# Two value tiles ahead of the branch, and another order of requests at the start of a decoder's last layer

## The chip, the cores and the metric

The kernel runs on one core of a Trainium2 chip. A core has a matrix engine (TensorE, PE in the profile), a vector engine (VectorE, DVE), a scalar engine (ScalarE, ACT), a programmable engine (GpSimd, POOL) and a sync engine (SyncE, SP). Each runs its own list of instructions in order and waits on semaphores for the others. SP, ACT and POOL also request transfers (DMA) between memory and the on-chip buffers. TensorE writes its results into eight banks of PSUM, from which ScalarE or VectorE must read them before a bank can be used again.

The metric is the device time of one launch in microseconds (us), lower is better. One of the launches was recorded by the hardware profiler; its times are what the profile shows.

## The reference

A decoder of two layers on a batch of 4 sequences with 512 positions and 256 features, everything in 32-bit floats. After each step the input is added and a layer normalisation follows.

```python
x = _layernorm(x + _L0_attn_ref(...))    # layer 0: a recurrence that learns on the fly
x = _layernorm(x + _L0_xattn_ref(...))   # attention over a context of 1601 positions
x = _layernorm(x + _L0_ffn_ref(...))     # 8 experts, the best two for each position
x = _layernorm(x + _L1_attn_ref(...))    # layer 1: causal self attention, 16 heads of 16
x = _layernorm(x + _L1_xattn_ref(...))   # attention over the context, 16 heads, rotary
x = _layernorm(x + _L1_ffn_ref(...))     # a feed-forward block with quantised weights
```

Of these the change touches the start of layer 1. There the self attention of a batch entry needs its keys, queries and values from x, and the cross attention needs, from the context, values and keys; the keys are rotated with two tables, a cosine and a sine:

```python
K = (key @ Wk.T + bk).reshape(b, sk, H, D).transpose(0, 2, 1, 3)
V = (value @ Wv.T + bv).reshape(b, sk, H, D).transpose(0, 2, 1, 3)
...
K = apply_rope(K, cos_k, sin_k)      # x * cos + x2 * sin, x2: neighbours swapped
...
scores = jnp.einsum('bqhd,bkhd->bhqk', Q, K) * SCALE
...
out = jnp.einsum('bhqk,bkhd->bqhd', attn, V)
```

The context does not depend on x, so its values and keys can be made at any time before the cross attention.

## The kernel before, in words

**The experts and the branch.** The experts of layer 0 run block by block in `run` (L1248), with side work (`attention_first`, L1158) that loads the weights of layer 1, the context of batch entry 0 (transposed, into the tiles `qt` and `ks`, which serve as store for it until they are needed), and two tiles `vself` for self-attention values, with columns of ones and zeros already set. A last function, `rest` (L1297), holds further blocks behind a condition on the number of expert rows (L1299); in this input the condition is false. Behind it comes a second condition with two versions of `last_layer` (L1311). So each engine passes two branches between the last expert block and layer 1.

**The start of the last layer** (L1952 to L1977) is written out by hand; within an engine the instructions keep the order of the program. In this order:

- the rows of the experts' results for batch entries 0 and 1 are gathered by POOL (L1371, 16 gathers);
- the 13 value tiles of batch entry 0 are made from the context (`context(0, (), range(4), ...)`): two products of 128 x 256 on TensorE into a PSUM bank, and a copy by ScalarE (L1506) into `vals[0]`. They are read when the cross attention begins;
- ScalarE loads its table for exponentials (L1963);
- the list `order` (L1973): the first two key products of entry 0 (`keys0[0:2]`, ScalarE adds a bias, L1492), the sum and the normalisation of x (`add`: VectorE's L1385, L165, L170, then ScalarE's L134, L136, L180), the key product `keys0[4]`, the transposes of x (`turn`: L1406, copied by ScalarE, L1409), the keys and queries of the first heads (`k0_`, `q0_`, L1431; they go to memory, through SP and ACT, L1340), the key product `keys0[5]`, and the rows of these keys and queries, fetched from memory in the layout of the scores (`rows0`, SP, L1343);
- the rotation of these four key tiles by VectorE (`turns0`), each with its store (L1340, `kcd<-raw`); the self-attention values of entry 0 (L1450); eight value tiles of entry 1.

**The units.** Then 32 units follow, one for each group of four heads of a batch entry, first the self attention of all entries, then the cross attention. A unit has a pass for the maxima of the scores (`slot1`, matmuls into tiles `most`, reduced by VectorE, L1588), which runs ahead of its main pass (scores L1627, exponentials on ScalarE L1637, weighted sums L1662). The maxima of a unit go through four small transfers (L1616, `qt<-nrows`) into the queries' rows. Other work is cut into pieces and slipped in between (`extras`). The first list (L1980) holds the second half of entry 0's keys and queries (`k1_`, `q1_`), the key products `keys0[2:4]`, `keys0[6]` and `keys0[7]` (rotated by POOL, L1459 to L1461), the stores still owed (`flush(0)`) and behind them the four rows of `rows1` (L1343), and value tiles of entry 1, whose context comes in chunks that ScalarE requests two ahead (`chunk`, L1471, L1476). Before unit 0's main pass SP requests the rotation tables (L2025 to L2027, `c_cos`, `c_sin`, 800.5 KB each).

**What orders the requests.** SP's list is strictly in order: a request that must wait holds up those behind it. In the compiled program the transfers of SP and ACT take turns on eight landing counters, in the order in which they stand in the program, both engines together. A request waits until the transfer that last used its counter, eight requests earlier, has landed.

```python
extras[0] = [
    k1_, q1_, *keys0[2:4], lambda: (keys0[6](), keys0[7]()), lambda: (flush(0), rows1()),
    *values1[8:11],
] + extras[0]
```

Of the kernel before, what the change touches and what calls it, by code (L numbers as in the profile page):

```python
# [9 lines left out]
F32 = mybir.dt.float32  # L10
# [7 lines left out]
P = 128  # L18
B, S, D = 4, 512, 256
S2 = 1601  # L20
NT = S // P
NKT = (S2 + P - 1) // P
# [3 lines left out]
NH, HD = 16, 16  # L26
# [4 lines left out]
MASKED = -float(2.0**100)  # L31
NLEV = 7
LEADX = 6
AHEAD = 20
PACE = 1.2
BOUNDED = 5000.0
# [7 lines left out]
def decoder(ctx: ExitStack, tc: tile.TileContext, a: dict, out: bass.AP):  # L44
    nc = tc.nc
# [16 lines left out]
    def bank():  # L62
        return psum["B"].tile([P, 512], F32, tag="bank", name="bank")
# [150 lines left out]
    def mm(ps, terms):  # L214

        n = len(terms)
        for i, (l, r) in enumerate(terms):
            nc.tensor.matmul(ps, l, r, start=(i == 0), stop=(i == n - 1))  # L218
# [52 lines left out]
    with (  # L271
# [248 lines left out]
        going, waiting, turn = [ttt(0)], [1, 2, 3], 0  # L520
# [283 lines left out]
    VW = HD + 1  # L804
# [4 lines left out]
    with tc.tile_pool(name="p2", bufs=2) as p2, ExitStack() as ordered:  # L809
# [102 lines left out]
        xaV = weight(p2, "xaV")  # L912
# [33 lines left out]
        for i in range(len(steps) + 1):  # L946
            if i + 1 < len(steps):
                b, t = steps[i + 1]
# [11 lines left out]
            if i > 0:  # L960
                b, t = steps[i - 1]
# [53 lines left out]
            pool.tile([P, n + 1], F32, tag=f"{name}{g}", name=f"{name}{g}")[:, :n] for g in range(NG)  # L1015
        ]

    def values_tile(pool, name, n, eng=nc.gpsimd):
        t = pool.tile([P, n, NH * VW + HD - 1], F32, tag=name, name=name)
        eng.memset(t[:, :, NH * VW :], 0.0)  # L1020
        heads = t[:, :, : NH * VW].rearrange("p k (h r) -> p k h r", r=VW)
        eng.memset(heads[:, :, :, HD : HD + 1], 1.0)
        return t


    with tc.tile_pool(name="p3", bufs=2) as p3, ExitStack() as ordered:
        W = {}
# [263 lines left out]
        run(blocks, more)  # L1291
        for _ in more:
            pass
        ordered.close()


# [14 lines left out]
    def last_layer(causal):  # L1311

        with ExitStack() as s4:
# [16 lines left out]
                ready[k] for k in ("diagq", "later", "qt", "ks", "nms", "vself")  # L1330
            )
            pv0 = s4.enter_context(tc.tile_pool(name="pv0", bufs=1, side="right"))
            vals = [values_tile(pv0, "v0", NKT, nc.vector)]
            kcross = [
                p4c.tile([P, S2 + 1], F32, tag=f"kc{i}", name=f"kc{i}")[:, :S2] for i in range(3)
            ]
# [128 lines left out]
            def flush(n):  # L1465
                while len(going) > n:
                    going.pop(0)()
# [14 lines left out]
            def context(b, keys, values, here=None):  # L1482


                def key(src, i, c, eng, apart=None):
                    if apart is None:
                        flush(1)
                    k0, kw = chunks[i]
                    ps = one()
                    mm(ps[:, :kw], [(W["xaK"][:, h, c * P : (c + 1) * P], src()[h][:, :kw]) for h in range(2)])  # L1490
                    raw = raw_tile()
                    nc.scalar.activation(raw[:, :kw], ps[:, :kw], AF.Identity, bias=ready["bk"][:, c : c + 1])  # L1492
                    turn = lambda: rotated(raw, kw, slice(k0, k0 + kw), eng, ready["turn", i] if here else None)
                    write = lambda: to_rows(kcd[b], c, k0, kw, raw[:, :kw])
                    if apart is None:
                        turn()
                        going.append(write)
                    else:
                        apart.append(lambda: (turn(), write()))

                def value(src, k):
                    kn, c0 = kn_of(k), (k % 4) * P
                    ps = one()[:, :D]
                    mm(ps[:kn], [(src()[c][:, c0 : c0 + kn], W["xaV"][:, c, :]) for c in range(2)])
                    dst = vals[b % 2][:kn, k, : NH * VW].rearrange("p (h r) -> p h r", r=VW)
                    nc.scalar.copy(dst[:, :, :HD], ps[:kn].rearrange("p (h r) -> p h r", r=HD))  # L1506

                items = []
                for i in sorted({*keys, *values}):
                    if here is None:  # L1510
                        src = lambda n=len(stream): chunk(n)
                        stream.append((b, i))
                    else:
                        src = lambda i=i: here[2 * i : 2 * i + 2]
                    eng = nc.gpsimd if here is None or i % 2 else nc.vector
                    if i in keys:
                        items += [
                            lambda *apart, s=src, i=i, c=c, e=eng: key(s, i, c, e, *apart) for c in range(2)
                        ]
                    if i in values:  # L1520
                        items += [lambda s=src, k=k: value(s, k) for k in range(4 * i, min(4 * i + 4, NKT))]
                return items
# [435 lines left out]
                f()  # L1958
            for f in fetch1:
                f()  # L1960
            for f in context(0, (), range(4), here=qt + kself):
                f()
            nc.scalar.preload_act_table_set(EXP_AND_LN)  # L1963


            keys0 = context(0, range(4), (), here=qt + kself)
            (k0_, q0_), rows0 = self_rows(
# [2 lines left out]
            (k1_, q1_), rows1 = self_rows(0, 1)  # L1970
            turns0 = []
            apart = lambda f: lambda: f(turns0)
            order = [apart(f) for f in keys0[0:2]] + add + [apart(keys0[4])] + turn + [k0_, q0_, apart(keys0[5]), rows0]  # L1973
            for f in order:
                f()
            for f in turns0 + self_values(0) + add1 + values1[:8]:
                f()  # L1977
            cosT, sinT = (p4c.tile([P, S2], F32, tag=n, name=n) for n in ("c_cos", "c_sin"))

            extras[0] = [  # L1980
                k1_, q1_, *keys0[2:4], lambda: (keys0[6](), keys0[7]()), lambda: (flush(0), rows1()),
                *values1[8:11],
            ] + extras[0]
            extras[1] = values1[11:] + keys1[:2] + extras[1]
# [27 lines left out]
            for i, u in enumerate(units):  # L2012
                for f in starts[i]:
                    f()
                nk = NKT if u[2] else NT
                work = extras[i]
                ran = 0
                while done["n"] < ends1[u] + lead(u):
                    reduces = [next1() for _ in range(min(2, ends1[u] + lead(u) - done["n"]))]
                    for f in reduces:  # L2020
                        f()
                    prepared()
                    if len(work) > nk // 2:
                        work.pop(0)()
                if i == 0:  # L2025
                    for t, name in ((cosT, "c_cos"), (sinT, "c_sin")):
                        nc.sync.dma_start(t, a[name])  # L2027
                ran = 0
                for k in range(nk):
                    due = (u, k - 1)  # L2030
                    if k == 0:
                        due = (units[i - 1], (NKT if units[i - 1][2] else NT) - 1) if i else None
                    pairs, reduces = [], []
                    for half in range(2):
                        shorter = causal and not u[2] and (k > 1) == (half == 1)
                        if shorter:
                            reduces.append([next1()] if i != 15 or done["n"] < ends1[units[16]] + LEADX else [])
                        pairs.append([scores(u, k, half, h) for h in range(2)])
                        if not shorter:
                            reduces.append([next1()] if i != 15 or done["n"] < ends1[units[16]] + LEADX else [])  # L2040
                        if 9 <= i < 16 and ahead and (i - 9) * NT + k >= PACE * (AHEAD - len(ahead)):
                            reduces[half].append(slot1(*ahead.pop(0)))
                        elif i == 15 and done["n"] < ends1[units[16]] + LEADX:
                            reduces[half].append(next1())
                        if u[2]:
                            exponents(u, k, half, pairs[half])
                            for f in reduces[half]:
                                f()
                            if quiet[i]:
                                quiet[i].pop(0)()  # L2050
                    if not u[2]:
                        for half in range(2):
                            if not causal:
                                diagonal(k, pairs[half])
                            exponents(u, k, half, pairs[half])
                            for f in reduces[half]:
                                f()
                            if quiet[i]:
                                quiet[i].pop(0)()
                    prepared()  # L2060
                    if k and u[2]:
                        weighted(*due)
                    while work and ran * nk < (k + 1) * (ran + len(work)):
                        f = work.pop(0)
                        f()
                        ran += 1
                        if f is pause:
                            break
                    if due and not (k and u[2]):
                        weighted(*due)  # L2070
                while work:
                    work.pop(0)()
                while quiet[i]:
                    quiet[i].pop(0)()
# [172 lines left out]
```

## Time and profile before

| | us |
|---|---|
| device time, three launches | 2027.69, 2021.38, 2018.23 |
| median | 2021.38 |
| profiled execution | 2012.39 |
| its span, first to last instruction | 2010.7 |
| mean granted TensorE clock | 0.99 |
| TensorE busy | 1967.9 (98%) |
| VectorE, ScalarE, POOL busy | 1139.6, 1065.1, 647.4 |
| last expert matmul to first matmul of the last layer | 860.90 to 865.21 |
| first score matmul of unit 0 (`most`) | 903.74 |

The times in the profile are counted from the start of the span. A row of a timeline has start, duration, engine, line, operation, what is written and read, the shapes, how many instructions are merged into the row, and in brackets how long the engine sat idle before it and what ended that. A row of the chain of waits has start, duration and what ran or was waited for. A busy TensorE is not a TensorE at its best: the granted clock (PEclk, 1.00 is full) tells how fast its matmuls run.

### The profile page before, as it was taken

How to read it: one execution, taken by the hardware profiler on the slowest of the kernel's cores; microseconds unless marked ns; L12 is line 12 of the kernel's file. 1: busy time of each engine (PE TensorE's matmuls, PEld its weight loads, DVE VectorE, ACT ScalarE, POOL GpSimd, SP SyncE). 2: the span in 40 equal slices, each digit the busy share in tenths (PEclk: the TensorE clock that was granted, in tenths of full speed). 3: DMA queues.
4: the chain of work that ended last, by engine and by line, in shares of the span. 5: the costliest groups of instructions: out<-in, count | busy, mean ns of one | idle time of the engine just before them, and what ended most of it. 6: DMA issues, size and time to landing. Idle time of an engine off the chain costs nothing.

```text
span 2010.7 us, 33740 instructions
## 1 busy us (share of the span) xinstructions
PE 1967.9 (98%) x12736; PEld 1221.4 (61%) x12736; DVE 1139.6 (57%) x2834; ACT 1065.1 (53%) x2241; POOL 647.4 (32%) x678
## 2 busy tenths in 40 slices
PE   9999999999999999988999999999999999999998
PEld 6768677788899999964455553333433333333366
DVE  3455334452243233356667887777777788887323
ACT  1111222224655555534555567788778788878721
POOL 3010001122222222233733344655655355353110
PEclk9999999999999999999999999999999999999999
DMA  9930411117887786743422110111210120102001
GB/s 366 358 106 1 166 66 54 51 64 278 331 309 278 260 324 261 291 118 117 129 74 66 54 61 28 56 38 48 77 45 29 35 87 18 33 18 85 1 11 34
DMA packets 80110, 242.61 MB, mean 121 GB/s; under 512 B 14135, under 2 KB 37085, under 8 KB 68029
## 3 DMA queue, kind: packets, MB, share of 16 engines
q1 hardware_dynamic: 59148, 141.86, 20.4%
q0 software_dynamic: 13152, 85.64, 11.2%
q10 hardware_dynamic: 7632, 12.80, 2.1%
q8 instruction: 105, 1.72, 0.3%
q14 instruction: 73, 0.59, 0.1%
HBM read 194.47 MB, written 56.69 MB: 125 GB/s over the span
## 4 chain that ended last, share of the span: by engine, by line
PE 50%; DVE 2%; POOL 1%; ACT 1%; DMA 1%; issue 1%; SPq 0%; ACTq 0%; POOLq 0%; DVEq 0%
PE s L1627 13%; PE one L218 12%; PE po L1662 12%; PE most L218 11%; PE one L1693 1%; DVE most L1588 1%; DVE pm L1586 1%; ACT x L180 0%; PE one L1718 0%; ACT ex L1637 0%; DMA kcd<-raw 0%; DVE st L165 0%; POOL raw L1459 0%; POOL swp L1460 0%; POOL raw L1461 0%
## 5 line engine op out<-in xcount | busy, mean ns | idle before, releaser
L1637 ACT ACTIVATE ex<-s 128x512 f32<-128x512 f32 (+4 forms) x1088 | 526.3, 565 | 159.3 <-PE most L218 101.0
L1586 DVE TENSOR_REDUCE pm<-most 128x1 f32<-128x512 f32 x768 | 478.7, 682 | 99.1 <-PE most L218 96.1
L218 PE MATMUL most<-kc,qt 32*128 32x512 f32 (+1 forms) x1920 | 399.4, 533 | 0.8 <-ACT ex L1637 0.2
L1627 PE MATMUL s<-qt,kc 32*128 32x512 f32 (+1 forms) x1560 | 382.0, 617 | 0.0
L1679 POOL TENSOR_TENSOR ot<-ot,part 128x512 f32<-128x512 f32 (+3 forms) x201 | 243.3, 1211 | 290.4 <-ACT part L1678 282.2
L1627 PEld LDWEIGHTS s<-qt,kc 32*128 32x128 f32 (+1 forms) x1560 | 125.0, 181 | 165.8 <-ACT ex L1637 125.5
L1662 PE MATMUL po<-ex,v 128*32 128x512 f32 (+1 forms) x1664 | 225.5, 606 | 0.2
L218 PEld LDWEIGHTS most<-kc,qt 32*128 32x128 f32 x1920 | 157.6, 184 | 45.5 <-issue 16.4
L1109 DVE TENSOR_TENSOR g<-g,sg 128x1024 f32<-128x1024 f32 (+1 forms) x38 | 45.5, 1197 | 214.0 <-ACT sg L1107 214.0
L1588 DVE CUSTOM_DVE_ANT_0 most<-most,c_diagq 128x384 f32<-128x384 f32 (+3 forms) x256 | 119.2, 516 | 45.9 <-PE most L218 44.8
L218 PE MATMUL wide<-xbT,eWg 128*128 128x128 f32 (+1 forms) x928 | 133.7, 304 | 1.5 <-ACT g L1107 1.5
L218 PE MATMUL wide<-xbT,eWi 128*128 128x128 f32 (+1 forms) x928 | 133.9, 304 | 0.0
L218 PE MATMUL bank<-eWo,g 128*128 128x256 f32 x592 | 130.8, 379 | 0.0
L218 PEld LDWEIGHTS wide<-xbT,eWi 128*128 128x128 f32 x928 | 124.9, 191 | 8.0 <-issue 1.1
L218 PEld LDWEIGHTS wide<-xbT,eWg 128*128 128x128 f32 x928 | 124.7, 192 | 8.3 <-ACT g L1107 1.7
L1662 PEld LDWEIGHTS po<-ex,v 128*32 128x32 f32 (+1 forms) x1664 | 34.5, 108 | 149.9 <-ACT ex L1637 145.9
L1678 ACT COPY part<-po 128x512 f32<-128x512 f32 (+3 forms) x201 | 114.4, 569 | 16.9 <-PE po L1662 15.0
L218 PEld LDWEIGHTS bank<-eWo,g 128*128 128x128 f32 x592 | 111.1, 190 | 14.3
L218 PE MATMUL most<-ks,qt 32*128 32x256 f32 (+3 forms) x512 | 95.0, 483 | 6.1 <-ACT v L1506 3.5
L711 POOL DMA_INDIRECT xs<-x,rows x32 | 31.3, 978 | 214.5 <-DVE ltot L697 173.9
L1627 PE MATMUL s<-qt,ks 32*128 32x128 f32 (+3 forms) x512 | 98.1, 482 | 0.9 <-DMA qt<-nrows 0.7
L1640 POOL TENSOR_SCALAR_AFFINE_SELECT ex<-ex 128x256 f32<-128x256 f32 x128 | 51.7, 408 | 128.2 <-ACT ex L1637 127.8
(339 smaller groups left out, 2974.9 us busy)
## 6 DMA issues: line engine op xcount, KB each, us to landing
xs<-zero SPq DMA_DIRECT2D x32, 512.0 KB
kc<-kcd SPq DMA_DIRECT2D x16, 800.5 KB
eWo<-in_eWo SPq DMA_DIRECT2D x8, 1408.0 KB
eWi<-in_eWi SPq DMA_DIRECT2D x8, 1028.0 KB
eWg<-in_eWg SPq DMA_DIRECT2D x8, 1028.0 KB
qt<-qd SPq DMA_DIRECT2D x31, 256.0 KB
ctxT<-in_ctxT SPq DMA_DIRECT2D x4, 1601.0 KB
kcd<-in_c_rowkc SPq DMA_DIRECT2D x4, 1601.0 KB
```

What stands on the lines that cost most here:

```text
L218: nc.tensor.matmul(ps, l, r, start=(i == 0), stop=(i == n - 1))
L711: nc.gpsimd.indirect_dma_start(xs, bass.IndirectOffsetOnAxis(ap=rows[:, k * NT + t : k * NT + t + 1], axis=0), x[b][:, t, :], None)
L1109: nc.vector.tensor_tensor(part, part, dst, ALU.mult)
L1586: nc.vector.tensor_reduce(pm[:, t, j, c : c + 1], ps, AX.X, ALU.max)
L1588: nc.vector.tensor_tensor_reduce(out=ps[:, :n], in0=ps[:, :n], in1=diagq[:, 384 - t * P : 384 - t * P + n], scale=1.0, scalar=LOWEST, op0= ...
L1627: nc.tensor.matmul(ps[:kn, q0:], kt[rows, k * P : k * P + kn], q2[rows, q0:], start=True, stop=cross or causal)
L1637: nc.scalar.activation(ex[:kn, h, q0:], ps[:kn, q0:], AF.Exp)
L1640: nc.gpsimd.affine_select(out=block, in_=block, pattern=[[0, 2], [1, P]], compare_op=ALU.is_ge, fill=0.0, base=0, channel_multiplier=-1,)
L1662: nc.tensor.matmul(po[j * 32 : j * 32 + 32, q0:], (vals if cross else vself)[b % 2][:kn, k, c0 : c0 + 32], ex[:kn, j % 2, q0:], start=True ...
L1678: nc.scalar.copy(part[:, q0:], po[:, q0:])
L1679: nc.gpsimd.tensor_tensor(state["ot"][:, q0:], state["ot"][:, q0:], part[:, q0:], ALU.add)
L1693: nc.tensor.transpose(pt[:, t * P : (t + 1) * P], ot[:, t * P : (t + 1) * P], ident)
```

## The change

There are four edits.

1. The first two value tiles of batch entry 0 (`SOON = 2`) are made at the end of the experts' stage, ahead of both branches, into the second `vself` tile. In the last layer SP copies them from there into `vals[0]`; the loop over value tiles and the memsets of `vals[0]` leave them out.
2. The key product `keys0[5]` moves ahead of the transposes of x, from behind the queries.
3. In the first list of extras the four rows of `rows1` are requested ahead of the stores that `flush(0)` still owes.
4. The rotation tables are requested by ScalarE, right behind its table load, and no longer by SP ahead of unit 0's main pass.

```diff
+SOON = 2
...
-    def values_tile(pool, name, n, eng=nc.gpsimd):
+    def values_tile(pool, name, n, eng=nc.gpsimd, first=0):
         t = pool.tile([P, n, NH * VW + HD - 1], F32, tag=name, name=name)
-        eng.memset(t[:, :, NH * VW :], 0.0)
-        heads = t[:, :, : NH * VW].rearrange("p k (h r) -> p k h r", r=VW)
+        eng.memset(t[:, first:, NH * VW :], 0.0)
+        heads = t[:, first:, : NH * VW].rearrange("p k (h r) -> p k h r", r=VW)
...
         run(blocks, more)
         for _ in more:
             pass
+
+        for k in range(SOON):
+            ps = bank()[:, :D]
+            mm(ps, [(ready["qt"][c][:, k * P : (k + 1) * P], W["xaV"][:, c, :]) for c in range(2)])
+            dst = ready["vself"][1][:, k, : NH * VW].rearrange("p (h r) -> p h r", r=VW)
+            nc.scalar.copy(dst[:, :, :HD], ps.rearrange("p (h r) -> p h r", r=HD))
         ordered.close()
...
-            vals = [values_tile(pv0, "v0", NKT, nc.vector)]
+            vals = [values_tile(pv0, "v0", NKT, nc.vector, SOON)]
...
-            for f in context(0, (), range(4), here=qt + kself):
+            nc.sync.dma_start(vals[0][:, :SOON, :], vself[1][:, :SOON, :])
+            for f in context(0, (), range(4), here=qt + kself)[SOON:]:
                 f()
             nc.scalar.preload_act_table_set(EXP_AND_LN)
-
+            cosT, sinT = (p4c.tile([P, S2], F32, tag=n, name=n) for n in ("c_cos", "c_sin"))
+            for t, name in ((cosT, "c_cos"), (sinT, "c_sin")):
+                nc.scalar.dma_start(t, a[name])
...
-            order = [apart(f) for f in keys0[0:2]] + add + [apart(keys0[4])] + turn + [k0_, q0_, apart(keys0[5]), rows0]
+            order = [apart(f) for f in keys0[0:2]] + add + [apart(keys0[4]), apart(keys0[5])] + turn + [k0_, q0_, rows0]
...
-            cosT, sinT = (p4c.tile([P, S2], F32, tag=n, name=n) for n in ("c_cos", "c_sin"))
...
-                k1_, q1_, *keys0[2:4], lambda: (keys0[6](), keys0[7]()), lambda: (flush(0), rows1()),
+                k1_, q1_, *keys0[2:4], lambda: (keys0[6](), keys0[7]()), lambda: (rows1(), flush(0)),
...
-                if i == 0:
-                    for t, name in ((cosT, "c_cos"), (sinT, "c_sin")):
-                        nc.sync.dma_start(t, a[name])
```

## The prediction

> **What bounds the kernel now.** I read the page first, then the stretch around the branch into the last layer: the view by stretches, the timelines of TensorE, ScalarE and SP, the chain of waits.
>
> ```profile
> PE 1967.9 (98%) x12736; PEld 1221.4 (61%) x12736; DVE 1139.6 (57%) x2834; ACT 1065.1 (53%) x2241; POOL 647.4 (32%) x678
> ```
>
> TensorE sets the span: a change gains only by taking instructions off it or closing one of its few holes. I cut the stretches at the steps of the clock (columns: us, then PE, PEld, DVE, ACT, POOL busy, PEclk, DMA share, GB/s):
>
> ```profile
> 862.75:866.17 3.42, 0.96 (x5) 0.89 (x6) 1.48 (x6) 0.06 (x1) 0.00 (x0) 1.00 0.14 46
> 866.17:869.58 3.41, 3.41 (x10) 2.70 (x9) 0.23 (x1) 0.74 (x2) 2.46 (x3) 0.50 0.44 81
> ...
> 883.23:886.64 3.41, 2.34 (x10) 1.24 (x10) 3.31 (x7) 3.41 (x7) 2.80 (x3) 1.00 0.41 114
> 886.64:890.06 3.42, 3.42 (x5) 1.35 (x4) 3.35 (x7) 0.30 (x2) 0.01 (x1) 0.50 0.13 40
> ...
> 924.19:927.60 3.41, 0.18 (x1) 0.18 (x2) 0.61 (x6) 0.60 (x2) 0.00 (x0) 1.00 0.88 250
> 927.60:931.02 3.42, 3.42 (x10) 1.55 (x13) 0.90 (x5) 3.03 (x9) 0.81 (x2) 0.50 0.98 361
> 931.02:934.43 3.41, 3.41 (x24) 1.61 (x16) 0.44 (x1) 1.41 (x4) 0.04 (x1) 0.50 0.65 250
> ```
>
> Three holes: at 863, 884 and 924. After each one the granted clock is 0.50 for one window of 3.41 us (twice after the third), in which 1.71 us of matmul time is lost. The first two, on TensorE's timeline:
>
> ```profile
> 865.21 8.83 PE L218 MATMUL one<-xaV,qt 128*128 128x256 f32 x32 [4.31 <-ACTq L1299]
> ...
> 881.63 1.88 PE L218 MATMUL one<-ks,xaK 128*128 128x512 f32 x4
> ...
> 886.34 3.51 PE L218 MATMUL one<-xT,qkvK 128*128 128x512 f32 x4 [0.28 <-ACT xT L1409]
> ```
>
> The last expert matmul ends at 860.90. TensorE then waits 4.31 us for ScalarE to come through the branch (L1299): ScalarE's last activation before it starts at 862.51 and its first semaphore behind it follows at 865.12, so crossing takes ScalarE 2.6 us. Between 883.51 and 886.34 TensorE has only eight transposes, and waits for this:
>
> ```profile
> 881.83 0.69 ACT L1492 ACTIVATE raw<-one,bk 128x512 f32<-128x512 f32 x1 [0.98 <-PE one L218]
> 882.41 0.29 ACT L134 ACTIVATE sd<-mv,eps 128x4 f32<-128x4 f32 x1
> ...
> 883.17 2.07 ACT L180 ACTIVATE x<-x,nb,rstd 128x256 f32<-128x256 f32 x4 [0.23 <-DVE nb L175]
> ```
>
> The moments of x are ready at about 879.5 (VectorE's L170 starts at 879.16 and takes 0.36); sd starts at 882.41 because ScalarE still works off value tiles and keys. The third hole, in the chain of waits:
>
> ```profile
> 917.95 3.80 DMA kcd<-raw
> ...
> 922.13 4.41 DMA kcd<-raw
> ...
> 926.56 0.40 ACTq L1476
> ...
> 927.00 0.38 ACT v L1506
> ...
> 927.42 1.07 PE most L218 x2
> ```
>
> ScalarE has finished its exponentials at 922.19. Its next step is a request for a context chunk (L1476), which may go out only when the transfer eight requests earlier has landed. On SP's timeline:
>
> ```profile
> 917.95 5.72 SPq L1340 DMA_DIRECT2D kcd<-raw  x4
> 923.76 0.42 SPq L1343 DMA_DIRECT2D ks<-ksd  x1
> 924.25 0.41 SPq L1343 DMA_DIRECT2D qt<-qd  x1
> ...
> 925.64 0.43 SPq L2027 DMA_DIRECT2D c_cos<-in_c_cos  x1
> 926.47 0.34 SPq L2027 DMA_DIRECT2D c_sin<-in_c_sin  x1
> ```
>
> Counting back eight from the chunk (c_sin, c_cos, four rows, the fourth store) gives the third of the four stores, requested at 922.13, landed at 926.54. Until then ScalarE and, through full PSUM banks, TensorE stand still (idle 3.48 us before 927.42).
>
> **The change part by part.** The sum is made against the profiled execution: 2012.39 us, span 2010.7. That is 9.0 under the median of the runs shown (2021.38), so I carry the difference over to the median.
>
> *Two value tiles ahead of the branch.* A tile is four matmul records at 0.215, 0.86 us at full clock: copies follow each other at 0.86 (875.80, 876.67, 877.53). Two tiles end at 860.90 + 1.72 = 862.62, inside the hole. ScalarE's two copies (0.37 each) stand behind sd at 862.51 to 862.80 and end about 863.55. Its branch now stands behind the second copy, which can start at 862.8 at the earliest: the crossing begins 0.3 to 1.0 later than 862.56. No row shows how far ahead of a running copy ScalarE takes a branch; since 862.56 lies inside the 0.29 us of the activation before it, I take +0.5, nearer the lower end. Behind the branch TensorE has 1.72 less. Net -1.2. A window at half clock after the shortened hole (865.7 - 862.6 = 3.1 us) I keep, as before.
>
> *The copy of these tiles.* Its 294 KB go out on SP behind two chunk requests (867.14, 867.59; 0.4 to 0.5 each). SP's next work is at 890.51, and the tiles are first read at 1205. Nothing; if they were late, only the cross units would see it. VectorE's two shorter memsets are 0.2 us beside idle time.
>
> *Tables requested by ScalarE.* Two requests of 0.40 stand behind the activation table load (878.78, 1.28 us) and before the first raw. If requests run beside a load, they cost 0; if not, 0.8 in front of raw. The chunk request at 900.46, issued inside a copy (900.39 to 900.76), says beside: 0. The 1.6 MB land within 8 us (before: requested 925.64, landed by 934.5, at up to 361 GB/s), so by about 887, beside gathers for batch 1 that VectorE needs at 891 or later and ahead of the row stores at 889. First use is at 949.65. Removing the two requests from SP is worth nothing on SP itself, whose next work was at 929.55.
>
> *The sixth key product ahead of the transposes.* ScalarE: raw 1 ends 1.2 earlier, sd at 881.2, x done at 884.0; then two raws (0.67 each), not one, and the first xT copy at 885.4: TensorE starts k at 885.9, 0.4 earlier than 886.34. TensorE ends the keys at 883.51 + 0.5 - 1.72 + 1.72 = 884.0 and has the transposes until 885.0: the hole shrinks from 2.83 us with eight transposes to 0.9. Behind q the product is gone: -1.72. The window at 0.50 (886.64) should go with the hole: -1.71; bounds 0 and -1.71. TensorE's busy share of that window was 0.69; other windows with 0.59 to 0.63 kept the full clock (115.2, 504.4, 978.8), two with 0.53 and 0.61 did not (1016.4, 1156.3). With a hole of 0.9 the share passes 0.73, and I take -1.71 whole. Stage: -0.4 - 1.7 - 1.7 = -3.8 by the first score matmul (903.74), which includes the -1.2. What is late next is the query rows: q's store would go at about 890.0 (before 892.39), land 4.7 us later, as its load shows (897.12), and the load needs another 2.5: 897.2, with the score matmul at 899.9.
>
> *Rows ahead of stores, tables out of the way.* The order becomes two stores, four rows, two stores, chunk. Eight back from the chunk is now the first store, requested at 917.95 and landed by 922.3. ScalarE gets on at 922.35, not 926.56: -4.2. The two windows at 0.50 lost up to 3.4 us, but ScalarE has 7.4 us of work between 927.0 and 936.15 and becomes the limit: 9.15 could shrink to 7.4. Bounds 0 and -1.75; I take -1.0. The rows go out at 921.8, when SP is past the second store (POOL's last product ends 921.14), and no longer at 923.76. They land some 3.2 later, the first pair by 926.5; TensorE wants it at 932.31 - 5.2 = 927.1. Left in their old place they would come 0.8 late. The stores moved behind them reach HBM some 1.5 later and are read first by the cross units. The requests for the next maxima (before 929.55) now wait for the second store and three rows, about 927; landed by 929.5, wanted at 939.09 - 5.2 = 933.9.
>
> Sum: -3.8 - 5.2 = -9.0. The profiled execution would take 2003.4; on the scale of the median, 2012.4.
>
> [...] By rows, 4.31 us without work were followed by a half-clock window, and so were 2.34 busy us of 3.41 (883.23). [...]
>
> **The rivals.**
> 1. No half-clock window behind the branch: the work is 1.71 us earlier, of which the moments (879.5, plus 0.5) let 1.1 through; and the third part gains its whole 1.75. Sum -9.0 - 1.1 - 0.75 = -10.9: 2001.5, or 2010.5. For it: the hole falls from 4.3 to 3.1. Against: the window at 883. Chance 0.20.
> 2. The third hole only moves: the first pair of rows lands late, or the chunk still waits for a late store. For it: the second store, 256 KB, took 4.4 us from request to landing, and the rows follow it in one queue. If the rows land at 930.5, 3.4 of the 5.2 is lost again, and if the second window at 884 also stays slow, -3.9 remains: 2008.5, or 2017.5. Chance 0.18.
> 3. Slower: the tables hold up the key stores. In the new order, by the count of eight, the first two stores wait for the tables to land, and SP's queue behind them holds two further stores, the next key rows and the first maxima. Each us that the tables land after 894.5 comes back as a us at the score matmuls. It decides against the change beyond 894.5 + 9 = 903.5, 25 us after the request; the trace has at most 8. Landing at 915, the price is 20 - 9 = +11: 2023, or 2032. Chance 0.10, most of it for what I have not seen.
>
> **How the numbers follow.** Forecast 0.52, rivals 0.20, 0.18, 0.10. Runs of one kernel scatter by 0.3%, and 0.5% (10.1 us) is about what a measurement here tells from no change. Faster by more than that: 0.24 of the forecast's 0.52, 0.14 from rival 1, 0.02 from rival 2, together 0.40. Within: 0.27 + 0.06 + 0.15 + 0.01 = 0.49. Slower: 0.11. The range reaches from rival 1 on the scale of the profiled execution, less 2.5, to rival 2 on that of the median, plus 6.5 (the highest run shown lies 6.3 over the median): 1999 to 2024.
>
> **What would show it.** The hole before the first value matmul in the last layer at about 3.1 us, ScalarE's first semaphore at about 865.6; eleven value tiles behind it; k's first matmul about 0.4 earlier with the clock at 1.00 after it; the first score matmul near 900; no wait of ScalarE's third chunk request, no idle of 3.4 us in unit 0, and clock 1.00 there. I am wrong if ScalarE's crossing grows by more than 1 us, if a store waits for a table, or if unit 2's first score matmul waits for its rows.

## The result and the profile after

| | before | after |
|---|---|---|
| device time, us, median (lowest to highest), 20 launches each | 2024.01 (2018.23 to 2031.06) | 2015.76 (2005.50 to 2024.03) |
| ratio, 95% interval | | 0.9955 (0.9943 to 0.9966) |
| profiled execution, us | 2012.39 | 2016.24 |

The change gains 8.3 us between the medians, 9.1 us by the ratio (0.0045 x 2024). But the two profiled executions show the opposite. The one of before lies below all 20 timed launches of before, and the one of after is 3.9 us longer. So they can't simply be subtracted, and most of what follows rests on further profiles of both kernels.

The page of after, busy time by engine (us, share of the span, instructions):

```profile
PE 1969.7 (98%) x12736; PEld 1220.9 (61%) x12736; DVE 1139.4 (57%) x2834; ACT 1064.3 (53%) x2241; POOL 647.4 (32%) x678
```

TensorE, 98% busy, still sets the span. The three holes, on TensorE's timeline of after (start, duration, work, and in brackets the idle time before it and what ended that):

```profile
868.72 7.11 PE L219 MATMUL one<-xaV,qt 128*128 128x256 f32 x24 [3.25 <-ACTq L1306]
...
893.61 3.78 PE L219 MATMUL one<-xT,qkvK 128*128 128x512 f32 x4 [2.44 <-ACT xT L1416]
...
934.25 1.14 PE L219 MATMUL most<-ks,qt 32*128 32x384 f32 x8 [1.94 <-DMA qt<-nrows]
```

The hole behind the branch is 3.25 us where it was 4.31. The wait for the transposes of x has grown from 0.28 to 2.44. The 3.48 us in unit 0 are gone, and 1.94 us before unit 2's first score matmul (L219, `most`) have come. The view by stretches of after, cut at the steps of the clock (us, then PE, PEld, DVE, ACT, POOL busy, PEclk, DMA share, GB/s), shows the clock behind each:

```profile
866.55:869.97 3.42, 1.25 (x6) 1.15 (x7) 0.85 (x4) 0.06 (x1) 0.55 (x1) 1.00 0.18 48
869.97:873.38 3.41, 3.41 (x10) 2.71 (x9) 0.48 (x1) 1.06 (x3) 2.50 (x4) 0.50 0.54 112
876.80:887.06 10.26, 10.21 (x32) 5.44 (x30) 4.27 (x13) 4.16 (x8) 6.68 (x8) 1.00 0.64 227
...
890.47:893.88 3.41, 0.97 (x5) 0.57 (x4) 3.34 (x8) 1.66 (x4) 0.29 (x1) 0.50 0.14 40
893.88:897.29 3.41, 3.41 (x5) 1.34 (x6) 3.31 (x7) 0.17 (x1) 0.00 (x0) 0.50 0.00 0
```

The stretch from 876.80 to 887.06 has full clock and a busy TensorE, and yet something is slow in it. ScalarE's timeline of after shows it, where ScalarE draws off key products:

```profile
883.75 0.69 ACT L1499 ACTIVATE raw<-one,bk 128x512 f32<-128x512 f32 x1 [0.51 <-PE one L219]
886.66 0.69 ACT L1499 ACTIVATE raw<-one,bk 128x512 f32<-128x512 f32 x1 [2.22 <-PE one L219]
```

The two products come 2.91 us apart; in before they came 1.67 apart (880.16, 881.83). The last value tiles come 1.44 apart (877.94, 879.38, 880.82), before 0.86. Both are a rate of about 0.6 (1.67 / 2.91, 0.86 / 1.44), although the clock is recorded as 1.00.

### The profile page after: what moved, and what is told of

Its sections match the earlier page's. It is cut to its first block, busy times and chain, and to the rows that moved or that the text cites. A ratio compares the mean times of both kernels' runs of the same rounds, so it can differ in the third digit from the quotient of the medians.

```text
span 2014.5 us, 33744 instructions
## 1 busy us (share of the span) xinstructions
PE 1969.7 (98%) x12736; PEld 1220.9 (61%) x12736; DVE 1139.4 (57%) x2834; ACT 1064.3 (53%) x2241; POOL 647.4 (32%) x678
## 3 DMA queue, kind: packets, MB, share of 16 engines
q8 instruction: 105, 1.72, 0.3%
## 4 chain that ended last, share of the span: by engine, by line
PE 50%; DVE 3%; POOL 2%; ACT 1%; issue 1%; DMA 1%; SPq 0%; ACTq 0%; POOLq 0%; DVEq 0%
PE s L1634 13%; PE one L219 12%; PE po L1669 12%; PE most L219 11%; DVE most L1595 1%; PE one L1700 1%; DVE pm L1593 1%; PE one L1725 0%; DVE st L166 0%; POOL raw L1466 0%; POOL swp L1467 0%; ACT x L181 0%; PE one L1413 0%; ACT ex L1644 0%; POOL raw L1468 0%
## 5 line engine op out<-in xcount | busy, mean ns | idle before, releaser
L219 PE MATMUL most<-kc,qt 32*128 32x512 f32 (+1 forms) x1920 | 399.5, 533 | 0.8 <-ACT ex L1644 0.2
L219 PEld LDWEIGHTS most<-kc,qt 32*128 32x128 f32 x1920 | 157.6, 184 | 46.0 <-issue 16.6
L219 PE MATMUL wide<-xbT,eWg 128*128 128x128 f32 (+1 forms) x928 | 133.7, 304 | 1.7 <-ACT g L1108 1.7
L219 PE MATMUL wide<-xbT,eWi 128*128 128x128 f32 (+1 forms) x928 | 133.9, 304 | 0.1
L219 PE MATMUL bank<-eWo,g 128*128 128x256 f32 x592 | 130.8, 379 | 0.0
L219 PEld LDWEIGHTS wide<-xbT,eWi 128*128 128x128 f32 x928 | 124.9, 191 | 8.2 <-issue 1.0
L219 PEld LDWEIGHTS wide<-xbT,eWg 128*128 128x128 f32 x928 | 124.6, 191 | 8.5 <-ACT g L1108 1.8
L219 PEld LDWEIGHTS bank<-eWo,g 128*128 128x128 f32 x592 | 111.1, 190 | 14.4
L219 PE MATMUL most<-ks,qt 32*128 32x256 f32 (+3 forms) x512 | 93.6, 481 | 4.2 <-DMA qt<-nrows 1.9
```

## The experiments

In the later series before takes 2011 to 2012 us and after 2004.4 to 2005.1; each ratio is against before in the same series. For the profiles I use one ruler. All times are us; it starts at the end of the last expert matmul, and the mark is the 115th first-pass score matmul (`most`, at 960.08 in the first profile of before). Columns: to the first matmul of the last layer, from there to k's first matmul, from there to the first score matmul, from there to the mark, and the sum.

| kernel (profile) | start | to k | to scores | to mark | sum |
|---|---|---|---|---|---|
| before, first | 4.31 | 21.13 | 17.40 | 56.34 | 99.18 |
| before, second | 4.33 | 21.98 | 17.40 | 56.17 | 99.89 |
| after, first | 5.34 | 24.89 | 15.80 | 53.12 | 99.16 |
| after, second | 5.09 | 19.98 | 13.99 | 52.28 | 91.33 |
| after, third | 5.29 | 19.97 | 13.99 | 51.37 | 90.62 |
| tiles only | 5.08 | 19.40 | 15.71 | 54.85 | 95.03 |
| key product only | 4.25 | 22.83 | 13.99 | 55.99 | 97.07 |
| rows and tables only | 4.47 | 22.04 | 17.40 | 52.25 | 96.17 |
| tables only | 4.53 | 21.78 | 15.71 | 50.83 | 92.84 |
| rows only | 4.22 | 21.13 | 15.71 | 55.74 | 96.80 |
| without the tiles | 4.51 | 21.70 | 13.99 | 53.00 | 93.20 |
| rows first | 5.34 | 20.06 | 13.99 | 51.28 | 90.67 |
| rows first, again | 4.98 | 19.98 | 13.99 | 49.84 | 88.79 |
| rows first, without the tiles | 4.31 | 22.37 | 13.99 | 49.89 | 90.56 |

Differences of 0.8 or 1.7 are matmuls at half clock. Behind the branch the 32 value matmuls take 8.83 us in the first profile of before and 9.69 in the second; k's four matmuls take 3.51 us at clock 0.50 in the first profile of before and 1.98 at 1.00 in the second of after. The clock record goes by windows on a grid of 3.41 us, and the work does not lie in them at the same place in every execution: from the end of the last expert matmul to the next window it is 1.85 us in the first profile of before (860.90, 862.75) and 3.17 in the first of after (863.38, 866.55). So I take one such window more or less as chance.

**What belongs to one execution.** The two kernels were run again unchanged.

> The kernel before, unchanged, for a second profile. Its first profiled execution took 2012.39 us, less than each of its 20 timed runs (2018.23 to 2031.06, median 2024.01). Theory 1 (the sum of the prediction holds for a usual execution too): a second profile that lies near 2020 is longer by the same few us in all stretches away from the change, and around it shows the same holes: 4.3 us behind the branch, 2.8 us at the transposes, 3.5 us in unit 0, each followed by a stretch at clock 0.50. Theory 2 (a usual execution of before has slow stretches around the change which its first profile lacked): between 860 and 930 us it is later by 3 us or more than the first profile, by further stretches at clock 0.50 or by ScalarE's key copies 2.9 us apart, where 1.7 us is usual.

> The changed kernel, unchanged, beside further variants and for a second profile. In the same series the single edits gave 0.9995 (tiles), 0.9989 (key product) and 0.9987 (rows and tables) of the kernel before. Theory 1 (the parts add up): 0.9971, 5.9 us of 2010.9. Theory 2 (the parts take the same wait away, so that less is left together): 0.998 or more, 4 us or less. Theory 3 (they open more together, as the first comparison said): 0.9955, 9 us. In the profile, the stretch from 876 to 893 of the first profile, where key copies stood 2.9 us apart, is gone if it belongs to one execution, and there again if it belongs to the change.

> The changed kernel once more, for a second measurement of its ratio beside the next two: 0.9971 if the last series holds, 0.9955 if the first comparison does. In the profile, from the end of the last expert matmul to the first score matmul 39.1 us as in the second after profile if that one was usual, 46.0 us as in the first if the slow stretch comes back.

Before again: 1.0005 (0.9994 to 1.0016), profiled execution 2011.57, sum 99.89. Theory 2 falls for this series: there is no slow stretch. Theory 1 holds in the main: the holes behind the branch and at the transposes are the same. Of the third hole only ScalarE's wait is there again (its request goes out 7.17 us behind the first score matmul of the main pass, 7.56 in the first profile); TensorE has little idle time in it:

```profile
927.77 1.22 PE L218 MATMUL most<-ks,qt 32*128 32x256 f32 x2 [0.68 <-ACT v L1506]
```

In this execution the clock is 0.50 from 921.43 on, before the hole, so slow matmuls fill the time in which the first profile shows 3.48 us of idle TensorE: four value matmuls take 2.08 us from 922.57, and 1.13 from 935.19. After: 0.9971 (0.9956 to 0.9986), the single edits added up, and then 0.9969 (0.9957 to 0.9981). The slow stretch did not come back. In ScalarE's timeline of the second after profile the key products are 1.72 apart again:

```profile
881.76 0.69 ACT L1499 ACTIVATE raw<-one,bk 128x512 f32<-128x512 f32 x1
883.48 0.69 ACT L1499 ACTIVATE raw<-one,bk 128x512 f32<-128x512 f32 x1 [1.03 <-PE one L219]
```

and TensorE's timeline has k right behind the transposes, at full clock (its four matmuls take 1.98 us, in the first profile 3.78):

```profile
868.58 7.11 PE L219 MATMUL one<-xaV,qt 128*128 128x256 f32 x24 [3.00 <-ACTq L1306]
...
886.71 1.04 PE L1413 MATMUL one<-ident,x 128*128 128x128 f32 x8
888.56 1.98 PE L219 MATMUL one<-xT,qkvK 128*128 128x512 f32 x4 [0.82 <-ACT xT L1416]
```

So the 2.44 us, the half clock at 890 and about 7 us up to the first score matmul belong to that one execution and not to the change. Two undisturbed after profiles need 8 to 9 us less from the last expert to the mark than before.

**The tiles ahead of the branch.** First alone, then everything but them.

```diff
+        for k in range(SOON):
+            ps = bank()[:, :D]
+            mm(ps, [(ready["qt"][c][:, k * P : (k + 1) * P], W["xaV"][:, c, :]) for c in range(2)])
...
+            nc.sync.dma_start(vals[0][:, :SOON, :], vself[1][:, :SOON, :])
-            for f in context(0, (), range(4), here=qt + kself):
+            for f in context(0, (), range(4), here=qt + kself)[SOON:]:
```

> Only the first edit: two value tiles ahead of the branch, their copy by SP. Theory 1 (the prediction's step): the last layer starts 0.5 us later and has 1.72 us less to do, -1.2 us in all, ratio 0.9994. Rival (the after profile read literally): ScalarE starts the last layer 0.9 us later and the clock windows behind the branch fall later, so that keys and transposes run slowly: 0 to +3 us, ratio 1.000 to 1.0015. If the whole gain of the change (8.3 us between medians) were here, the ratio would be 0.996.

> The second, third and fourth edits without the first (no tiles ahead of the branch). Theory 1 (the parts add up): 0.9976 of before, and the changed kernel 0.0005 better than it. Rival (the tiles cost something where the rest is done, as the first after profile read): it is 1 us or more faster than the changed kernel, 0.9966 or less.

Alone 0.9995 (0.9985 to 1.0005); all but the tiles 0.9970 (0.9956 to 0.9984), against 0.9971 with them in the same series. The times can't tell the tiles from nothing. The profiles can. The last layer starts 5.19 us after the last expert matmul with the tiles (mean of six profiles) and 4.37 without (mean of eight): 0.82 later, with 1.72 less to do, -0.9. By k's first matmul the difference is larger: 25.2 us after the last expert matmul with the tiles and 26.7 without (means of four and three undisturbed profiles with the second edit), and 24.5 and 26.0 (one and five profiles without it), so -1.5. The rest lies in the clock: five of the eight profiles without the tiles have two half-clock windows at the branch (their 32 value matmuls take 9.48 to 9.93 us, those of the other three 8.83), the six with them one (24 value matmuls in 7.10 or 7.11 us). The prediction's -1.2 lies between the two, and all of them are below what these times resolve. No rival loss shows: "all but the tiles" is not faster by 1 us.

**The key product.**

```diff
-            order = [...] + add + [apart(keys0[4])] + turn + [k0_, q0_, apart(keys0[5]), rows0]
+            order = [...] + add + [apart(keys0[4]), apart(keys0[5])] + turn + [k0_, q0_, rows0]
```

> Only the second edit: the sixth key product ahead of the transposes. Theory 1 (the prediction's step): the transposes have product work beside them, k starts where it did, the product of 1.72 us is gone behind q and the half-clock stretch after the transposes with it: up to -3.4 us by the first score matmul, ratio 0.998 to 0.999. Rival: the product runs 1.72 us ahead of the transposes and delays x (ScalarE must draw it off first), and the half-clock stretch stays: 0 to -1 us, ratio 0.9995 to 1.000.

0.9989 (0.9978 to 0.9999), 2.2 us. From k to the scores it is 13.99 us in all kernels with this edit but the disturbed one, against 17.40 or 15.71 without it: 1.72 is the product, and the other 1.7 is a half-clock window which comes in three of the six profiles without the edit (k's four matmuls take 3.51 to 3.59 us in these, 1.98 or 1.99 in the other three). The product now lies in front of k, which starts 27.1 us after the last expert matmul, against 25.4 to 26.5 (mean 26.0) without either edit. So k does not start where it did, as theory 1 had it, but 1.1 us later: that much of the rival is true. By the first score matmul it is 41.1 us against a mean of 42.7, so -1.6. Behind the queries theory 1 holds, with the window worth half of what it was given.

**Rows and tables, together and apart.**

```diff
-                k1_, q1_, *keys0[2:4], lambda: (keys0[6](), keys0[7]()), lambda: (flush(0), rows1()),
+                k1_, q1_, *keys0[2:4], lambda: (keys0[6](), keys0[7]()), lambda: (rows1(), flush(0)),
...
+            for t, name in ((cosT, "c_cos"), (sinT, "c_sin")):
+                nc.scalar.dma_start(t, a[name])
...
-                if i == 0:
-                    for t, name in ((cosT, "c_cos"), (sinT, "c_sin")):
-                        nc.sync.dma_start(t, a[name])
```

> Only the third and fourth edits: rows ahead of the owed stores, tables requested by ScalarE. Theory 1 (the prediction's step): ScalarE's third chunk request no longer waits for a store, -4.2 us, and with the shorter half-clock stretch -5.2 us, ratio 0.9974. Rival 1 (the after profile): unit 2's first score matmul then waits about 2 us for its rows and a half-clock stretch follows, so that -3.2 us is left, ratio 0.9984. Rival 2: the whole 8.3 us between the medians come from here, ratio 0.996.

> The fourth edit alone: the rotation tables requested by ScalarE behind its table load, the rows still behind all four stores. By the counters the third chunk request then waits for the first store instead of the third. Theory 1: the counter is the whole of the third hole, the wait of 4.2 us at the chunk request is gone, and ratio and profile are those of both request edits together (0.9987). Rival: with the rows in their old place they are late, unit 2's first score matmul waits 1 to 3 us for them and a stretch at clock 0.50 follows: 0.9990 to 1.000.

> The third edit alone: the four rows ahead of the owed stores, the tables still on SP in their old place. By the counters the third chunk request then waits for the first of the four rows instead of the third store. Theory 1 (the wait is set by the counter): the row is requested when SP is past the second store, about 921.8 on the scale of the first before profile, and lands about 3.2 later, at 925.0; ScalarE gets on 1.5 us earlier than 926.56 and no more: 0.9993 of before, and the wait at the chunk request is there, shorter. Rival (the order of the rows is the gain, the counter is not): as much as both request edits together, 0.9987 or less.

Together 0.9987 (0.9975 to 0.9999), tables alone 0.9981 (0.9968 to 0.9994), rows alone 1.0004 (0.9993 to 1.0015). ScalarE's timeline with the tables alone:

```profile
920.45 2.06 ACT L1637 ACTIVATE ex<-s 128x512 f32<-128x512 f32 x4 [3.56 <-PE s L1627]
922.50 0.39 ACTq L1476 DMA_DIRECT2D cx<-in_ctxT  x1
922.93 0.37 ACT L1506 COPY v<-one 128x256 f32<-128x256 f32 x1 [0.41 <-PE one L218]
```

and with the rows alone:

```profile
919.49 2.06 ACT L1637 ACTIVATE ex<-s 128x512 f32<-128x512 f32 x4 [3.40 <-PE s L1627]
926.82 0.38 ACTq L1476 DMA_DIRECT2D cx<-in_ctxT  x1
927.24 0.37 ACT L1506 COPY v<-one 128x256 f32<-128x256 f32 x1 [5.69 <-DMA ks<-ksd]
```

With the tables gone from SP, the request goes out as the exponentials end. By then the first store, now eight requests earlier, has landed too, 3.16 us behind the first score matmul of the main pass; the request goes out at 3.18. It is this landing that times the request: in the variant below which requests the rows first, it goes out 1.95 us behind that matmul, while the exponentials still run. With the rows alone it stands 5.3 us behind them, and the profile now names the transfer that the count of eight named: the first row, `ks<-ksd`. The chain of waits of that kernel has its size:

```profile
921.23 5.57 DMA ks<-ksd
...
926.82 0.38 ACTq L1476
...
927.24 0.38 ACT v L1506
...
927.67 0.72 PE most L218 x2
```

The row took 5.57 us, not the 3.2 of the expectation, so not even 1.5 us were gained. By the landing counters this is so wherever the rows stand between the stores: the first row takes 5.55 to 5.65 us in those six profiles and 3.16 to 3.33 in the five with the rows behind all stores. It is requested 1.9 us sooner and lands about 0.5 us later, so the third edit does not bring the rows sooner. What makes them slower there was not separated. Measured from the first score matmul of the main pass (`s`), the chunk request goes out 7.56 and 7.17 us later in before, 8.46 with rows alone, 3.18 with tables alone, and 3.29, 3.33 and 3.33 in the three after profiles. By these times the counter is the whole of ScalarE's wait, and moving the tables alone lifts it; from the scores to the mark TensorE then needs 50.83 us, against 56.34 and 56.17 in before. In the landing records the requests of SP and ACT use eight counters in turn, 100 to 107: in the first profile of before the chunk waits for 103, which the third store moves last at 926.54, and goes out at 926.56; in the first after profile it waits for 104, which the first store moves last at 927.98, and goes out at 928.00. The rival's other half, late rows, did not decide: with the tables alone TensorE waits 1.17 us before unit 2's first score matmul, and the profile puts that to ScalarE.

**The rows ahead of all stores.** In the first after profile, SP's timeline has the rows behind a store that waits for POOL:

```profile
923.63 3.81 SPq L1347 DMA_DIRECT2D kcd<-raw  x2
927.53 0.41 SPq L1350 DMA_DIRECT2D ks<-ksd  x1
928.00 0.59 SPq L1350 DMA_DIRECT2D qt<-qd  x1
```

Their second transfer, requested at 928.00, landed at 934.12, and unit 2's first score matmul starts at 934.25; the profile put that wait to a maxima transfer (`qt<-nrows`) whose counter moved 0.01 us later. Without the tiles this wait is there too, by name (`qt<-qd` are the rows), on TensorE's timeline and in the chain of waits:

```profile
926.59 0.93 PE L218 MATMUL most<-ks,qt 32*128 32x384 f32 x8 [1.84 <-DMA qt<-qd]
```

```profile
920.45 6.01 DMA qt<-qd
...
926.59 0.93 PE most L218 x8
```

The variant keeps all four stores back until the rows are requested. Then it was run again, and once without the tiles.

```diff
-                        flush(1)
+                        flush(9 if kept else 1)
...
-                k1_, q1_, *keys0[2:4], lambda: (keys0[6](), keys0[7]()), lambda: (rows1(), flush(0)),
+                k1_, q1_, lambda: (kept.append(1), keys0[2]()), keys0[3],
+                lambda: (keys0[6](), keys0[7](), kept.clear()), lambda: (rows1(), flush(0)),
```

> The changed kernel with the four rows of the second head pair requested ahead of all four stores of the rotated keys, not between the second and the third. In the first after profile SP stood 3.8 us at the second store for POOL's product before it came to the rows, and unit 2's first score matmul waited 1.94 us for them, with 3.4 us at clock 0.50 behind it. Theory 1 (the rows are what is late next): this wait goes, and 2 to 3.6 us with it: 0.9982 to 0.999 of the changed kernel. Rival (ScalarE limits there, or the clock stretch comes anyway): the wait goes and nothing else, 0.9995 to 1.000 of the changed kernel.

> The changed kernel with the rows ahead of all four stores, once more. The last series gave 0.9961 of before, 0.9990 of the changed kernel, with intervals that overlap. Theory 1 (rows were what is late next): 1 to 3 us under the changed kernel again. Rival (that was scatter): equal within 1 us.

> The rows ahead of all four stores, with the second and fourth edit, and without the two tiles ahead of the branch. Theory 1 (the prediction's first step, 1.2 us for the tiles): 1.2 us over the kernel with the tiles. Rival (the tiles are worth nothing, as the last series had it: 0.9970 without and 0.9971 with them): equal to it or faster.

SP's timeline of the variant:

```profile
917.38 0.38 SPq L1350 DMA_DIRECT2D ks<-ksd  x1
...
918.75 0.42 SPq L1350 DMA_DIRECT2D qt<-qd  x1
919.28 4.79 SPq L1347 DMA_DIRECT2D kcd<-raw  x4
```

The rows are out right behind the maxima, and TensorE has no wait for them in any of the three profiles. From the scores to the mark they need 51.28, 49.84 and 49.89 us, against 53.12, 52.28 and 51.37 in the three after profiles. In time: 0.9961 (0.9948 to 0.9974) where after had 0.9971, then 0.9968 (0.9957 to 0.9980) where after had 0.9969, and without the tiles 0.9963 (0.9950 to 0.9976). Neither the 2 to 3.6 us of the first expectation nor the 1 to 3 us of the second were confirmed. No variant beats the changed kernel by more than its interval, and the one without the tiles is as fast as the one with them.

## Why the prediction was right

The forecast was 2012.4 us, -9.0 us and 0.45%. The first series gave 2015.76 us, inside the range, -8.3 us by the medians and -9.1 by the ratio. By their ratios the later two gave -5.8 and -6.2 us (0.0029 and 0.0031 of 2011 and 2012), with an interval of 2.4 to 3 us to each side. Point by point:

- **Tiles ahead of the branch, -1.2.** Mechanism right, one term left out. ScalarE's branch comes 2.13 us behind the last expert matmul in all six profiles with the tiles, 1.62 in the eight without: 0.5 later, as forecast. Yet the last layer starts 0.8 later, so -0.9 by the start alone. The term left out is TensorE's own branch. In the first profile of before it takes 3.34 us from 856.9, beside the expert matmuls; with the tiles it begins at the tiles and takes 3.45 to 3.81 us, so it ends near ScalarE's, and in the third after profile it ended last (`PEq L1306`, 3.20 us of idle time). The hole is 3.0 to 3.25 us in the three after profiles and the forecast was 3.1; the later start is hidden there, as the tiles also end later than forecast, 2.09 us behind the last expert matmul and not 1.72.
- **Copy by SP and tables by ScalarE, nothing.** Right. In the second after profile the table requests stand at 880.51 and 880.88, inside the table load (880.42, 1.28 us), and the next key product is drawn off at 881.76, as soon as the load is over.
- **Key product, -3.8 by the first score matmul, the tiles included.** From the end of the last expert to the first score matmul: before 42.84, the undisturbed after profiles 39.06 and 39.25, so -3.8 and -3.6 against the forecast's own profile. Moved by the 2.59 us by which the second after profile's experts end later, the forecast puts the first score matmul at 899.9 + 2.6 = 902.5; it was 902.55. Against the mean of the five profiles without either edit (42.71) it is -3.6. The half-clock window at the transposes, which was taken as lost every time, comes in only three of six profiles without the edit. Against the forecast's own profile the terms come out one by one: k starts 0.4 earlier in the second after profile, and from k to the scores 3.4 us are gone. For the key product alone they leave 2.6 us (3.8 less the tiles' 1.2); it gave 2.2 by the times and 1.6 by its profile.
- **Rows ahead of stores, tables out of the line, -5.2.** The shift of ScalarE's request is right to a tenth: 922.35 was forecast, 3.35 after the first score matmul of the main pass, and it was 3.3. But it comes from the tables alone; the prediction took both edits together. The step that failed is the one that put these 4.2 us on TensorE's path in full. The five profiles with both edits and the rows in the changed place need 52.4 us on average from the scores to the mark, and the four without either 55.8: -3.4. TensorE's own work in that stretch, taken at full clock, is 47.0 to 48.2 us in all fourteen profiles. The rest is idle time, which falls from 3.7 to 2.5 us on average, and the loss at half clock (half of the busy time in windows at 0.50), which falls from 4.5 to 2.4. So the windows gave more than the 1.0 forecast, and the hole far less than 4.2, for two reasons. TensorE's hole was 3.48 us in the forecast's own profile, and in two of the four profiles slow matmuls fill it (0.68 and 0.70 us of idle time). And in two of the five there is a new wait of 1.8 to 1.9 us before unit 2's first score matmul. The prediction had the rows landing 0.6 us ahead of need and called their lateness the point where it would be wrong; in those two profiles it was, and in all five the first pair of rows takes 5.6 to 6.1 us to land, not 3.2. The forecast of clock 1.00 in unit 0 failed too: each of the five has one or two windows at 0.50. In three of them they begin 1.6 to 2.6 us behind the first score matmul of the main pass, so it is not the third hole that brings them.
- **The sum.** -3.6 up to the scores and -3.4 behind them make -7.0, between the series (-6 and -9). Of the 2.0 us that are missing, 0.2 lie in the first part and 1.8 in the second. That the first series came out at -8.3 and -9.1, so near to the forecast, is luck as far as the later series and these profiles tell.

Of the rivals, the first (no half-clock window behind the branch) fell: all six profiles with the tiles have a hole of 2.89 to 3.25 us there and a window at 0.50 behind it, although TensorE was busy for 0.4 to 1.3 us of the window before. The second (the third hole only moves) is half true, by the wait before unit 2. The third (tables hold up key stores) did not happen: SP's first four key stores take 2.98 us in the second after profile and 4.58 with rows and tables alone, against 4.21 and 3.96 in the two profiles of before.

What stays open is the size of the first series. Before took 2024 us there and 2011 later, and after spread over 18.5 us there and over 6 to 9 later. At a recorded clock of 0.990 after took 2010 to 2019 us there and 2007 in the second series. So something slowed executions there which the clock record does not show. The later series ran on chips 15, 14 and 14; the chip of the first is not on record, so a difference between chips is not ruled out. The first after profile has a stretch of that kind; that it is the same cause is argued, not shown.

## What to carry to other kernels

Where a request stalls, count the requests between it and the transfer at whose landing it goes on: here it was the eighth before (landed at 926.54, request at 926.56). Two requests taken out of that line lifted ScalarE's whole wait of 4.2 us, and a mere change of order among them only moved it to another transfer (the first row, 5.57 us). What that is worth was bounded by the idle time and the slow time of the engine that sets the span, not by the length of the wait: 3.4 us were gained. Check also whether an engine's own branch lies hidden beside work that the change moves, as TensorE's 3.34 us did here. Where holes are followed by half-clock windows that fall elsewhere in each execution, a gain of one such window (1.7 us here) is half chance in any single profile (three of six at the transposes): compare stretches over several profiles, and price the window at its frequency. A few us between two profiled executions prove nothing when the timed launches of one kernel spread over 10 (before in the first of the later series: 2004.76 to 2014.49).

## What the hardware showed that was not expected

- TensorE delivered results at about 0.6 of its rate (2.91 us for a key product instead of 1.72, 1.44 for a value tile instead of 0.86) for some 10 us while its clock was recorded as 1.00 and its matmuls as back to back. The slow copies begin at 876.73, at the edge of a window of the clock's grid (876.80). It was seen once.
- The granted clock goes with much of the scatter: over 35 launches of before in the first of the later series, the two at 0.987 took 2013.9 us (median) and the two at 0.994 took 2005.2. The clock was halved behind holes shorter than a window of 3.41 us; the shortest at the branch was 2.89 us (rows first, again), with 0.30 us for each of the 24 value matmuls behind it and 0.22 for the 20 that follow. How long TensorE was busy in a window does not settle it: at the transposes 2.34 us of 3.41 were followed by half clock in both profiles of before, and 2.32 with the tables alone were not; at the start of the main pass 2.74 were in one profile of before and 2.75 in the other were not. Of eight profiles without the tiles, five had two half-clock windows at the branch; the six with them had one.
- Between the stores, the first of the four rows took 5.55 to 5.65 us to land, with or without the tables on SP, where the forecast had 3.2.
